# A second PSUM bank for row work in two layers, and a last group with tiles of its own

## The chip, the cores and the metric

The kernel runs on one core of one Trainium2 chip. The metric is the device time of one execution in microseconds. Its engines are TensorE (PE: matmuls, and PEld its weight loads), VectorE (DVE), ScalarE (ACT), GpSimd (POOL) and SyncE (SP, which issues the loads). PSUM is the memory that matmuls write[...].

## The reference, cut to what matters

Four graph layers work on the same 4096 nodes with 64 features and the same dense 4096 x 4096 matrix of zeros and ones. Each layer is added to its input and layer-normed.

```python
# layer 0: mean of neighbours, linear map, relu, normalize
z = concat([x, (adj @ x + x) / (rowsum(adj) + 1)]) @ W + b
x = layernorm(x + normalize(relu(z)))
# layers 1 and 3: attention between all pairs in hyperbolic space
att = sigmoid(left[:, None] + right[None, :] + b) * adj
x = layernorm(x + proj(expmap(x, einsum('ij,ijd->id', att, logmap(x_i, x_j)))))
# layer 2: each row's last neighbours with weights halving from the right
rank = cumsum(adj, axis=1); deg = rank[:, -1:]; k = minimum(deg, 100)
pos = rank - (deg - k)
w = adj * where(pos > 0, 0.5 ** (k - pos), 0)
x = layernorm(x + w @ (x @ weight) + bias)
```

A layer needs all rows of the one before it, since every row sums over all columns.

## The kernel before, in words

**Tiling.** The function `stream` works on groups `s` of 1024 rows (WW), from the last (3) to the first (0): GROUPS. Against each group it streams the matrix in 16 loads of 1 MB (`load`, L685; six buffers, issued by SP), each with two blocks of 128 columns, also from the last to the first. So each layer has 64 loads and reads the matrix once. In layer 2 the first pass (`wide_pass`) takes groups 3 and 2 together, and two `narrow_pass` take 1 and 0.

**Pair work and row work.** Pair work is what is done for every block against a group. In layer 0: matmuls into four `acc` banks (L1354), and on VectorE the test that the matrix holds only zeros and ones, one for every second load (`check`, L824), which also holds the load's buffer. In layers 1 and 3 (`attend`): three matmuls for each z half (L1045, L1048, L1051), a Sigmoid and a Square on ScalarE (L1060, L1063), two products on VectorE (L1066, L1068), and sums on PE (L1023). In layer 2: counts on PE (L1502), an Exp on ScalarE (L1509), sums on PE (L1514).

Row work is what happens to a group once its sums are there: turning them to rows, norms, the next layer's operands. It is written as generators: `end_0` and `end_2` end layers 0 and 2 (with `norm_rows` and `prepare` behind them), `move` ends layers 1 and 3, `linear` makes x @ W for layers 0 and 2 (L1207 turns x, ScalarE copies it, L1218 multiplies, then VectorE or ScalarE takes the result), `spread_left` lays out the left logits.

**Order of issue.** Generators wait in two queues. `tick(n)` is called after every step of pair work and lets each queue issue its next step; a step yields the number of ticks until the next. `need(tag)` ticks without pair work until something is done; layer 2 calls it before each quarter of the columns, since `supports` of that quarter (halves, L1228 and L1229) come from `linear(2, s)`. In layers 0 and 2 (`manual_schedule(engines=FIXED)`) PE and ScalarE keep the order in which the program issues; VectorE, POOL and SP there, and all engines in layers 1 and 3, are ordered by a planner that simulates with its own costs and takes the first instruction that is ready, the earlier issued one if there are several. In layers 1 and 3 `mark` (L597) keeps row work behind the pair work issued before it, from the second group on, until the last group's pairs are issued.

**The bank of row work.** Every matmul of row work writes a tile of the pool `aux`, which has one bank: `take` (L665) gets it and notes it in `held`; a step that has read it pops `held`; `free` (L670) makes other generators wait in the order of issue until nobody holds it. Even so the next writer waits on the chip for the last reader. In layer 0 six more banks are in use. Later the pool `ps` has three z tiles of two banks and one `acc` bank; in layer 2's wide pass two z tiles hold counts, and both halves of the third (`both`, L1445) the sums, while the `acc` bank is idle.

**The move.** `move` (L1084) is a chain of some 100 small instructions on 128 x 8 numbers with a few on 128 x 512. `Small` (L714) puts the small ones on POOL for all groups but the last, and on VectorE for the last. The products w = x * u (L1109) and x * p (L1193) are on POOL for every group. All groups share the row tiles: numbers such as `k`, `d`, `uu`, the big ones `w_att`, `sq` and `u_1`, one buffer each. In layer 3 `store` (L1533), a DMA issued on ScalarE, follows each group; the store of group 1 is issued in the same tick as the first step of group 0's move. After the last store nothing is left but a check of the input's form, which is done earlier.

Of the kernel before, what the change touches and what calls it, by code (L numbers as in the profile page):

```python
# [10 lines left out]
F32 = mybir.dt.float32  # L11
F16 = mybir.dt.float16
# [5 lines left out]
PSUM = bass.MemoryType.PSUM  # L18

P = 128  # L20
N = 4096
D = 64
NB = N // P
W = 512
# [7 lines left out]
WB = WW // P  # L32
# [26 lines left out]
def gnn_stack_kernel(  # L59
# [15 lines left out]
    nc = tc.nc  # L75
    V = nc.vector
# [11 lines left out]
    for src, at in ((b0, 0), (b2, D), (b_att1, 2 * D), (b_att3, 2 * D + 1), (r1, 2 * D + 2)):  # L88
        n = src.shape[0]
# [479 lines left out]
    def stream(fits):  # L569

        with ExitStack() as st:
# [7 lines left out]
            row = pool("f_row")  # L579
# [34 lines left out]
            def tick(n):  # L614
                for _ in range(n):
                    place[1] += 1
                    mark(False)
                    for queue in queues:
                        while queue and queue[0][1] <= place[1]:
                            wait = next(queue[0][0], None)  # L620
                            if wait is None:
                                queue.pop(0)
                                continue
                            queue[0][1] = place[1] + wait
                            if wait:
                                break
                    mark(True)

            def later(steps, second=False, wait=0):
                queues[second].append([steps, place[1] + wait])  # L630
# [30 lines left out]
            def pool_done(small, large=0):  # L661

                return 2 + int(small * 0.33 + large)

            def take(dtype, *shape):  # L665

                held.append(1)
                return aux.tile(list(shape), dtype, name="aux")

            def free():  # L670
                while held:
# [4 lines left out]
            def x_of(layer):  # L676

                if layer not in layers_x:
                    layers_x[layer] = xs.tile([P, NB, D], F32, name="x")
                return layers_x[layer]  # L680
# [10 lines left out]
            def grp(name, bufs=None):  # L691
                kw = {"bufs": bufs} if bufs else {}
                return row.tile([P, WB, D], F32, name=name, **kw)

            def nums(name, n=WB):
                return row.tile([P, n], F32, name=name)

            def over(v):
                return v[:, :, None].to_broadcast([P, v.shape[1], D])
# [14 lines left out]
            class Small:  # L714


                def __init__(self, on_pool):
                    self.on_pool = on_pool
                    eng = nc.gpsimd if on_pool else V
                    self.ts, self.mul = eng.tensor_scalar, eng.tensor_mul  # L720
                    self.add, self.sub = eng.tensor_add, eng.tensor_sub

                def stt(self, out, in0, scalar, in1, op0, op1):
                    if not self.on_pool:
                        V.scalar_tensor_tensor(out, in0, scalar, in1, op0, op1)
                        return
                    t = nums("pool_t")
                    nc.gpsimd.tensor_scalar(t, in0, scalar, None, op0)
                    nc.gpsimd.tensor_tensor(out, t, in1, op1)

# [3 lines left out]

                def rsqrt(self, a, name, small):

                    r, t = nums(name), nums("rs_t")
                    if self.on_pool:
                        yield self.wait(small)
                    V.tensor_scalar(  # L740
                        r.bitcast(I32), a.bitcast(I32), -0.5, float(0x5F3759DF),
                        ALU.mult, ALU.add,
                    )
                    for _ in range(3):
                        self.mul(t, r, r)
                        if self.on_pool:
                            self.mul(t, t, a)
                            self.ts(t, t, -0.5, 1.5, ALU.mult, ALU.add)
                            self.mul(r, t, r)
                        else:  # L750
                            self.stt(t, t, -0.5, a, ALU.mult, ALU.mult)
                            self.stt(r, t, 1.5, r, ALU.add, ALU.mult)
                    return r
# [330 lines left out]
            def move(layer, s, sums, curve):  # L1084
# [4 lines left out]
                least = 1e-15 if layer == 1 else 1e-30  # L1089
                at = blocks(s)  # L1090
                xg, x2g = x_of(layer)[:, at, :], x2[:, at]
                k, d, uu = nums("k"), nums("d"), nums("uu")
                w, sq = grp("w_att"), grp("sq")

                all_u = row.tile([P, WB, D + 1], F32, name="u_1")
                u, sum_1 = all_u[:, :, :D], all_u[:, :, D]
                for part in range(2):
                    yield from free()
# [7 lines left out]
                    )  # L1106
                    held.pop()
                    yield near()
                nc.gpsimd.tensor_mul(w, xg, u)  # L1109
                nc.scalar.activation(sq, u, AF.Square)  # L1110

                G = Small(s != GROUPS[-1])
                yield G.wait(0, 1) if G.on_pool else near()
                V.tensor_reduce(uu, sq, AX.X, ALU.add)
                yield soon()
# [73 lines left out]
                G.stt(p, p, 1.0, r, ALU.add, ALU.mult)  # L1189
                G.mul(q, q, r)  # L1190
                yield soon()
                E = nc.gpsimd if G.on_pool else V
                nc.gpsimd.tensor_mul(w, xg, over(p))  # L1193
                E.tensor_mul(u, u, over(q))
                yield soon()
                yield soon()
# [56 lines left out]
            with ExitStack() as lp:  # L1253
                own = lp.enter_context(tc.tile_pool(name="m0_own", bufs=1))
                sb = lp.enter_context(tc.tile_pool(name="m0_sb", bufs=2))
                ps = lp.enter_context(tc.tile_pool(name="m0_ps", bufs=6, space=PSUM))

                first = own.tile([P, NB, 2 * D], BF16, name="first")
                third = own.tile([P, NB, D + 1], BF16, name="third")
# [78 lines left out]
                with tc.manual_schedule(engines=FIXED):  # L1338
                    for s in GROUPS:
# [42 lines left out]
                        if s > 0:  # L1382
                            own_of = linear(0, s - 1, w0_sb[:D, :], own_part)
                            later(in_turn((0, s - 1), own_of))


            place[0] = 1
            sb = pool("p_sb", 2)
# [2 lines left out]
            def z_tile():  # L1391
                return ps.tile([P, WW], F32, name="z", bufs=3)
# [27 lines left out]
            def end_2(s, sums):  # L1420
                z = grp("z0")
                yield 1
                yield from free()
                t = to_rows_of(sums)
                yield 1
                V.scalar_tensor_tensor(
                    z.rearrange("p (h k) f -> p h k f", h=2)[:, 0], t[:, 0], 2.0**CUT / SUP,
                    b2_sb[:, None, :].to_broadcast([P, SB, D]), ALU.mult, ALU.add,
                )
                V.scalar_tensor_tensor(  # L1430
                    z.rearrange("p (h k) f -> p h k f", h=2)[:, 1], t[:, 1], 2.0**CUT / SUP,
                    b2_sb[:, None, :].to_broadcast([P, SB, D]), ALU.mult, ALU.add,
                )
                held.pop()
                yield 1
                V.tensor_add(z, z, x_of(2)[:, blocks(s), :])
                yield 1
                yield from norm_rows(3, s, z, x2[:, blocks(s)])
                yield from prepare(3, s, att3, batt3_sb, curve3, 1e-30, good[:, 1], 40)

            def wide_pass(two):

                zs = [z_tile() for _ in two]

                both = z_tile()  # L1445
                accs = [both[:, :W], both[:, W:]]
                behind, lag = [None, None], []
                for g in reversed(range(NB // 2)):
                    edges = [load_2(s, g) for s in two]
                    need((2, 2 * g // WB))  # L1450
                    for k in (1, 0):
                        j = 2 * g + k
                        w = sb.tile([P, 2, WW], F32, name="sq").bitcast(BF16)[:, :, :WW]
                        for i, edge in enumerate(edges):
                            here = edge[:, k * WW : (k + 1) * WW]
                            count(zs[i], behind[i], here, j, WW)
                            behind[i] = here
                            weights_of(zs[i], WW, w[:, i])
                            if i == 1:
                                for of, acc in enumerate(accs if lag else ()):  # L1460
                                    add_up(acc, *lag[of])
                                lag = [(j, w[:, n, :W], w[:, n, W:]) for n in range(2)]
                            if two[0] != GROUPS[0] or j < BLOCKS[4]:
                                tick(1)
                for of, acc in enumerate(accs):
                    add_up(acc, *lag[of])
                return accs
# [43 lines left out]
            def add_up(acc, j, *ws):  # L1511
                for part in range(2):
                    for h, w in enumerate(ws):
# [4 lines left out]
                            stop=j == BLOCKS[-1] and part == 1,  # L1518
                        )

            with tc.manual_schedule(engines=FIXED):

                for some in (GROUPS[:2], GROUPS[2:3], GROUPS[3:]):
                    accs = wide_pass(some) if len(some) == 2 else narrow_pass(some[0])
                    for s, acc in zip(some, accs):
                        sums = row.tile([P, W], F32, name="sums", bufs=2)
                        nc.scalar.copy(sums, acc)
                        later(end_2(s, sums))


            place[0] = 3
# [91 lines left out]
```

## Time and profile before

| | us |
|---|---|
| median of three runs | 1134.94 |
| lowest, highest | 1126.09, 1137.0 |
| the profiled execution | 1138.77 |
| its span | 1137.0 |
| PE, VectorE, ScalarE, POOL busy in it | 1027.5, 909.9, 802.1, 277.8 |

PE is busy for 90% of the span, VectorE for 80%, ScalarE for 71% and POOL for 24%. A line of a timeline has the start and the duration in us, the engine, the source line, the operation, what it writes and reads, and in brackets the engine's idle time before it and what ended it. ACTq stands for an instruction that ScalarE only issues, such as a DMA. Busy time of PE is modelled, and its matmuls overlap.

### The profile page before, as it was taken

What the parts mean: (1) busy time and instruction counts of PE and PEld (TensorE: products, weight loads), DVE (VectorE), ACT (ScalarE), POOL (GpSimd) and SP (SyncE); (2) the same over time, 40 slices, a digit from 0 to 9 for tenths busy, and PEclk for the clock granted to TensorE, in tenths of its full rate; (3) what the DMA queues carried; (4) which work ended last, traced back from release to release, by engine and by line L of the source; (5) the groups of instructions that cost most, each with busy time, mean ns of one, the idle gap of its engine ahead of it and who ended that gap; (6) DMA issues with size and microseconds to landing.
All of it is one profiled execution on the core that took longest, in us unless ns stands there. A gap on an engine that the chain in (4) does not pass through costs nothing.

```text
span 1137.0 us, 13841 instructions
## 1 busy us (share of the span) xinstructions
PE 1027.5 (90%) x4949; PEld 406.2 (36%) x4949; DVE 909.9 (80%) x1450; ACT 802.1 (71%) x896; POOL 277.8 (24%) x649
## 2 busy tenths in 40 slices
PE   5998989789999999998989998789899999999960
PEld 2554555233333333332334323223233333333320
DVE  6577976999999999989354494544999999999964
ACT  0003122989989889986755778889899999998940
POOL 0011101010145244315400020000101444345282
PEclk9989998899999999999988999799999999999985
DMA  9999999546666566553967987478546766766300
GB/s 345 395 372 385 358 416 358 184 148 223 208 236 222 185 223 221 190 210 125 367 222 262 361 274 274 145 272 286 195 158 218 253 222 199 253 219 215 133 1 22
DMA packets 38421, 271.60 MB, mean 239 GB/s; under 512 B 4550, under 2 KB 4550, under 8 KB 5574
## 3 DMA queue, kind: packets, MB, share of 16 engines
q1 hardware_dynamic: 37440, 269.50, 65.6%
q10 hardware_dynamic: 902, 1.12, 0.3%
q8 instruction: 41, 0.67, 0.2%
q14 instruction: 38, 0.31, 0.1%
HBM read 269.55 MB, written 1.05 MB: 238 GB/s over the span
## 4 chain that ended last, share of the span: by engine, by line
PE 59%; DVE 23%; ACT 8%; POOL 4%; DMA 3%; issue 2%; ACTq 0%; SPq 0%; POOLq 0%; DVEq 0%
PE acc L1023 14%; PE z L1502 9%; DVE t L1068 7%; PE z L1045 7%; DVE t L1066 6%; PE z L1051 6%; PE z L1048 6%; PE acc L1354 6%; PE z L1514 3%; DMA edges<-in_adj_dram 3%; ACT sq L1063 3%; PE acc L1514 2%; ACT sq L1509 2%; DVE junk L824 2%; ACT sig L1060 1%
## 5 line engine op out<-in xcount | busy, mean ns | idle before, releaser
L1066 DVE SCALAR_TENSOR_TENSOR t<-z,sig 128x1024 f32<-128x1024 f32 x256 | 309.6, 1219 | 16.8 <-ACT sq L1063 10.2
L1063 ACT ACTIVATE sq<-z,turn 128x1024 f32<-128x1024 f32 x256 | 278.0, 1112 | 43.8 <-PE z L1051 18.3
L1068 DVE SCALAR_TENSOR_TENSOR t<-sq,t 128x2048 f32<-128x2048 f32 x128 | 296.5, 2316 | 0.4
L1060 ACT ACTIVATE sig<-left_b,right 128x1024 f32<-128x1024 f32 x256 | 286.0, 1147 | 3.1 <-DVE t L1066 2.7
L1023 PE MATMUL acc<-t,xe 128*64 128x512 f32 x1024 | 258.6, 612 | 16.1 <-DVE t L1068 15.9
L1045 PE MATMUL z<-edges,two_i 128*128 128x512 bf16 x512 | 201.2, 393 | 6.6 <-DVE t L1066 6.6
L1051 PE MATMUL z<-dst,src 74*128 74x512 f16 x512 | 195.4, 382 | 0.0
L1048 PE MATMUL z<-lo_hi,hi_lo 128*128 128x512 f16 x512 | 194.4, 380 | 0.0
L1509 ACT ACTIVATE sq<-z,at_edge 128x512 bf16<-128x512 f32 (+1 forms) x192 | 149.9, 829 | 49.2 <-PE z L1502 46.6
L824 DVE SCALAR_TENSOR_TENSOR t<-edges 128x2048 bf16<-128x2048 f32 x32 | 73.1, 2289 | 59.2 <-DMA edges<-in_adj_dram 59.0
L1023 PEld LDWEIGHTS acc<-t,xe 128*64 128x64 f32 x1024 | 64.2, 137 | 146.7 <-issue 86.9
L1502 PE MATMUL z<-edges,pass_by 128*128 128x512 bf16 x248 | 91.5, 409 | 19.3 <-ACT sq L1509 19.3
L1354 PE MATMUL acc<-edges,first 128*128 128x512 bf16 x256 | 84.0, 411 | 13.2 <-DMA edges<-in_adj_dram 13.1
L1045 PEld LDWEIGHTS <-two_i 128*128 128x128 bf16 x512 | 50.4, 98 | 125.8 <-issue 81.2
L1502 PE MATMUL z<-edges,enter 128*128 128x512 bf16 x256 | 92.6, 404 | 0.0
L1354 PE MATMUL acc<-edges,third 128*65 128x512 bf16 x256 | 83.0, 407 | 0.0
L824 DVE SCALAR_TENSOR_TENSOR junk<-edges 128x2048 bf16<-128x2048 f32 x32 | 73.1, 2286 | 5.3 <-DMA edges<-in_adj_dram 5.1
L1051 PEld LDWEIGHTS <-src 74*128 74x128 f16 x512 | 49.2, 96 | 70.0 <-issue 8.0
L1048 PEld LDWEIGHTS <-hi_lo 128*128 128x128 f16 x512 | 50.4, 98 | 57.5 <-issue 12.1
L1109 POOL TENSOR_TENSOR w_att<-x,u 128x512 f32<-128x512 f32 x8 | 14.4, 1798 | 183.1 <-ACT u L1104 183.1
L855 POOL TENSOR_TENSOR sq<-z 128x512 f32<-128x512 f32 x8 | 14.1, 1757 | 180.3 <-DVE z L854 159.7
L1212 ACT COPY x_t<-aux 64x512 f32<-64x512 f32 x16 | 9.2, 576 | 59.2 <-PE aux L1207 59.2
(333 smaller groups left out, 1017.5 us busy)
## 6 DMA issues: line engine op xcount, KB each, us to landing
edges<-in_adj_dram SPq DMA_DIRECT2D x256, 1024.0 KB, 5.0
x<-in_x_dram SPq DMA_DIRECT2D x4, 256.0 KB
out_dram<-x ACTq DMA_DIRECT2D x4, 256.0 KB
w_sb<-in_L_gnn_W_dram ACTq DMA_DIRECT2D x1, 32.0 KB, 4.7
given<-in_L_gnn_b_dram ACTq DMA_DIRECT2D x1, 0.2 KB
given<-in_L_gnn_bias_dram ACTq DMA_DIRECT2D x1, 0.2 KB
given<-in_L_gnn_b_att_dram ACTq DMA_DIRECT2D x1, 0.0 KB
given<-in_L_gnn_att_b_dram ACTq DMA_DIRECT2D x1, 0.0 KB
```

The costliest lines, as they stand in the source:

```text
L824: V.scalar_tensor_tensor(junk, a, 0.0, a, ALU.not_equal, ALU.not_equal, accum_out=odd[:, n : n + 1])
L1023: it = nc.tensor.matmul(acc[h * D : (h + 1) * D, :], xe[:, j, :], t[:, k, h * W : (h + 1) * W], start=j == BLOCKS[0], stop=j == BLOCKS[-1],)
L1045: nc.tensor.matmul(half, two_i, edge[:, at : at + W], start=True, stop=False)
L1048: nc.tensor.matmul(half, hi_lo[:, of], lo_hi[:, to], start=False, stop=False)
L1051: last = nc.tensor.matmul(half, src[:, of], dst[:, to], start=False, stop=True)
L1060: nc.scalar.activation(sig, left_b, AF.Sigmoid, bias=right[:, j : j + 1])
L1063: nc.scalar.activation(sq[:, k], zp, AF.Square, bias=turn, scale=-1.0 / UNIT)
L1066: V.scalar_tensor_tensor(t[:, k], zp, 0.0, sig, ALU.max, ALU.mult)
L1068: V.scalar_tensor_tensor(t, sq, HIGH**2, t, ALU.add, ALU.mult)
L1354: nc.tensor.matmul(accs[h][:m], lhs[:, j, :], edge[:, at : at + W], start=j == BLOCKS[0], stop=j == BLOCKS[-1],)
L1502: nc.tensor.matmul(z[:, h : h + W], lhs, rhs[:, h : h + W], start=j == BLOCKS[0], stop=True, skip_group_check=True,)
L1509: nc.scalar.activation(w, z[:, :n], AF.Exp, bias=at_edge, scale=-LN2)
```

## The change

Three things are changed.

1. `take` alternates between `aux` and a second bank, where the list `spare` holds one. In layer 0 that is a new pool `m0_aux` of one bank. In layer 2 it is the second half of a z tile, `third_z`, that is kept through the layer; its first half takes the sums of the second group of the wide pass, and those of the first go to the `acc` bank. `spare_ends` ticks until nothing is held and goes back to one bank; it stands at the end of layers 0 and 2. `free` and `held` stay as they were.
2. The small numbers of a move go through `G.nums`, which gives the last group a set of its own (suffix `_1`). Its big tiles are `y` and `xw` in place of `w_att` and `sq`, and in layer 3 the storage of `ys` in place of `u_1` (all three are used in `prepare`, which is over by then).
3. In the last group's move the two products that stood on POOL are on VectorE.

```diff
+            spare, turn_of = [], [0]
             def take(dtype, *shape):
                 held.append(1)
-                return aux.tile(list(shape), dtype, name="aux")
+                turn_of[0] += 1
+                if not spare or turn_of[0] % 2:
+                    return aux.tile(list(shape), dtype, name="aux")
+                return spare[0](dtype, shape)
+
+            def spare_ends():
+                while held:
+                    tick(1)
+                spare.clear()
...
+                last = s == GROUPS[-1]
+                G = Small(not last, "_1" if last else "")
+                E = V if last else nc.gpsimd
+                nums = G.nums
                 k, d, uu = nums("k"), nums("d"), nums("uu")
-                w, sq = grp("w_att"), grp("sq")
-                all_u = row.tile([P, WB, D + 1], F32, name="u_1")
+                w, sq = (grp("y"), grp("xw")) if last else (grp("w_att"), grp("sq"))
+                if last and layer == 3:
+                    all_u = ys.rearrange("p k f -> p (k f)").bitcast(F32)[:, : WB * (D + 1)]
+                    all_u = all_u.rearrange("p (k f) -> p k f", f=D + 1)
+                else:
+                    all_u = row.tile([P, WB, D + 1], F32, name="u_1")
...
-                nc.gpsimd.tensor_mul(w, xg, u)
+                E.tensor_mul(w, xg, u)
                 nc.scalar.activation(sq, u, AF.Square)
...
-                E = nc.gpsimd if G.on_pool else V
-                nc.gpsimd.tensor_mul(w, xg, over(p))
+                E.tensor_mul(w, xg, over(p))
                 E.tensor_mul(u, u, over(q))
...
+                rest_ps = lp.enter_context(tc.tile_pool(name="m0_aux", bufs=1, space=PSUM))
+                spare.append(
+                    lambda dtype, shape: rest_ps.tile(list(shape), dtype, name="aux_2")
+                )
...
-                both = z_tile()
-                accs = [both[:, :W], both[:, W:]]
+                accs = [ps.tile([P, W], F32, name="acc"), third_z[:, :W]]
...
+            third_z = z_tile()
+
+            def of_third(dtype, shape):
+                t = third_z[:, W:]
...
             with tc.manual_schedule(engines=FIXED):
+                spare.append(of_third)
                 for some in (GROUPS[:2], GROUPS[2:3], GROUPS[3:]):
...
+                spare_ends()
```

`of_third` returns that half in the shape and type asked for. Layer 0's loop ends with `spare_ends()` too.

More of the change, by code (lines that the diff above doesn't have):

```diff
@@ L714, in stream, with __init__ @@
             class Small:
-                def __init__(self, on_pool):
-                    self.on_pool = on_pool
+                def __init__(self, on_pool, suffix):
+                    self.on_pool, self.suffix = on_pool, suffix
                     eng = nc.gpsimd if on_pool else V
@@ L721, in __init__, with nums @@
                     self.add, self.sub = eng.tensor_add, eng.tensor_sub
+                def nums(self, name):
+                    return nums(name + self.suffix)
                 def stt(self, out, in0, scalar, in1, op0, op1):
@@ L726, in stt @@
                         return
-                    t = nums("pool_t")
+                    t = self.nums("pool_t")
                     nc.gpsimd.tensor_scalar(t, in0, scalar, None, op0)
@@ L735, in rsqrt @@
                 def rsqrt(self, a, name, small):
-                    r, t = nums(name), nums("rs_t")
+                    r, t = self.nums(name), self.nums("rs_t")
                     if self.on_pool:
@@ L1108, in move @@
                     yield near()
-                nc.gpsimd.tensor_mul(w, xg, u)
+                E.tensor_mul(w, xg, u)
                 nc.scalar.activation(sq, u, AF.Square)
-                G = Small(s != GROUPS[-1])
                 yield G.wait(0, 1) if G.on_pool else near()
@@ L1519, in add_up @@
                         )
+            third_z = z_tile()
+            def of_third(dtype, shape):
+                t = third_z[:, W:]
+                if dtype == F16:
+                    return t.bitcast(F16)
+                n = int(np.prod(shape[1:]))
+                if len(shape) == 2:
+                    return t[:, :n]
+                names = "abc"[: len(shape) - 1]
+                return t[:, :n].rearrange(
+                    "p (%s) -> p %s" % (" ".join(names), " ".join(names)),
+                    **dict(zip(names, shape[1:])),
+                )
             with tc.manual_schedule(engines=FIXED):
+                spare.append(of_third)
                 for some in (GROUPS[:2], GROUPS[2:3], GROUPS[3:]):
@@ L1528, in stream @@
                         later(end_2(s, sums))
+                spare_ends()
             place[0] = 3
```

## The prediction

> **What bounds the kernel now.** I read the stage table first (columns: stretch, then busy time and instruction count of PE, weight loads, DVE, ACT, POOL; TensorE clock, DMA share, GB/s). Layer 0 runs to about 187 us, layer 2 from 525 to 783, the tail from 1102.
>
> ```profile
> 143.00:187.00 44.00, 39.03 (x240) 22.36 (x239) 37.45 (x109) 8.33 (x16) 6.68 (x9) 1.00 0.97 385
> 525.00:645.00 120.00, 110.26 (x578) 43.63 (x578) 60.66 (x126) 75.35 (x78) 20.95 (x53) 0.93 0.71 265
> 1102.00:1137.00 35.00, 2.99 (x11) 1.95 (x9) 14.13 (x83) 2.18 (x5) 10.79 (x30) 0.50 0.05 18
> ```
>
> Layer 0 is a DMA stage (share 0.97, so PE's gaps there are mostly cover), layer 2's first pass a PE stage (110 of 120 us), and the last 35 us belong to nobody: one serial chain. The timeline of the tail shows the hole in it.
>
> ```profile
> 1102.83 1.23 PE L1102 MATMUL aux<-centre,sums 128*128 128x130 f32 x4 [0.68 <-ACT sums L1074]
> ...
> 1110.66 1.18 POOL L1197 TENSOR_TENSOR x<-u,w_att 128x512 f32<-128x512 f32 x1
> 1111.87 0.34 ACTq L1534 DMA_DIRECT2D out_dram<-x  x1
> 1112.25 0.38 ACT L1104 COPY u<-aux 128x260 f32<-128x260 f32 x1 [9.47 <-POOL x L1197]
> ...
> 1114.36 0.63 ACT L1110 ACTIVATE sq<-u 128x512 f32<-128x512 f32 x1
> 1114.47 1.17 POOL L1109 TENSOR_TENSOR w_att<-x,u 128x512 f32<-128x512 f32 x1 [2.63 <-ACT u L1104]
> ...
> 1115.68 0.69 DVE L1116 TENSOR_REDUCE d<-w_att 128x8 f32<-128x512 f32 x1 [0.60 <-POOL w_att L1109]
> ```
>
> The last group's sums are turned at 1104.06, but ScalarE takes them out at 1112.25, when the group before it has ended on POOL. Two things stand there at once: `u_1` is still that group's, and that group's store (L1534) is ahead in ScalarE's queue. The other place is in layer 2, where `need` runs row work with no pair work between:
>
> ```profile
> 578.23 0.71 PE L1102 MATMUL aux<-centre,sums 128*128 128x130 f32 x4
> 579.46 0.63 PE L1207 MATMUL aux<-ident,x 128*64 128x128 f32 x4 [0.52 <-ACT u L1104]
> 580.76 0.71 PE L1102 MATMUL aux<-centre,sums 128*128 128x130 f32 x4 [0.67 <-ACT x_t L1212]
> 581.94 1.10 PE L1218 MATMUL aux<-w_sb,x_t 64*128 64x64 f32 x8 [0.47 <-ACT u L1104]
> 584.30 0.63 PE L1207 MATMUL aux<-ident,x 128*64 128x128 f32 x4 [1.26 <-DVE halves L1229]
> 585.60 1.97 PE L1218 MATMUL aux<-w_sb,x_t 64*128 64x64 f32 x8 [0.67 <-ACT x_t L1212]
> 587.50 1.04 PE L1502 MATMUL z<-edges,pass_by 128*128 128x512 bf16 x2
> ```
>
> Every step waits for the reader of the single `aux` bank. A block normally takes 2.90 us here (the exponentials start every 2.90), yet 578.30 to 592.38 passes for one block: 11.2 us lost. A second such burst (613.0 to 623.7, need of group 0) loses 10.7 − 2.9 = 7.8.
>
> [...]the copy of `u` ends at 579.41, L1207 starts at 579.46. [...]Here the same eight L1218 matmuls take 1.10 us, then 1.97 after the waits[...]. [...]POOL's L1162 took 2.19 us beside an L1068 where its like take 0.20.
>
> **The change, part by part.** The sum is made against the profiled execution (1138.77 us, span 1137.0, 1.8 around it). The median shown is 1134.94, 3.8 lower; I subtract the saving from the median.
>
> *Tail (layer 3, last group).* Own `_1` numbers, `y`, `xw` and `ys` instead of `w_att`, `sq`, `u_1` remove the wait for group 1's POOL work, if the copies also come ahead of its store. Then: first copy 1104.1 to 1104.5; L1102 again 1.24 (still one bank here) to 1105.75; copy 0.38, Square 0.63 to 1106.8; the product on DVE beside it (0.69 as L1194); two reductions 0.69 + 0.60 to 1108.1. From `k` to `q` the trace takes 1116.87 to 1129.70 = 12.83, unchanged on DVE: 1121.0. Then two products and the sum on DVE, 3 x 0.65: 1123.0, where 1132.04 stands. **Saved: 9.0.** The POOL products removed (1.17 and 1.56 us) are in it. What is late next is still this chain: group 1's POOL chain ends at 1111.85, hidden under it[...]; its third L740 on DVE (1104.60) is due before the new work arrives. Group 0's store and the 5 us behind x stay.
>
> *Burst at 578.* Same instructions with two alternating banks. L1102 to 578.95; L1207 at once to 579.6; L1102 needs the first copy (done 579.4) to 580.3; L1218 to 581.4; L1207 to 582.05; its copy 0.58; L1218 waits for that and for DVE's reading of its bank (about 583.0), 1.10 at full clock; 10.3 us of the trace's work to block end becomes 8 matmuls' 1.9 + 0.98: 587.0. Bounds: 2 (clock still halves) to 5.4 (592.4 − 587.0). I take **4.5**. DVE's `d`, which held the halves back behind POOL's product to 583.2, is ready earlier as well.
>
> *Burst at 613.* Only the wait of 0.93 for DVE's halves is a bank wait; those of L1218 for x_t are data. If PE keeps its clock, L1218 saves 0.87 and the next eight L1502 1.35: together 3.2; if not, 0.9. I take **2.0**.
>
> *Layer 0.* Bank waits of PE sum to some 8 us (L929 after L1317 four times at 0.8, L941 1.6, L1207 1.0 and others). But the last group's 16 loads arrive at 1 MB per 2.7 us from 143.27, so the last lands near 183.8, and PE's last work ends at 186.3. **0.5**, bounds −4 to 4.5. Below nothing because VectorE's order may change (see the slower rival).
>
> *Layer 2, what is added.* Its `acc` bank now takes half of the first pass, where two halves of a z tile did. The first L1514 (533.39 now) must wait for layer 1's last sums, copied at 538.02, and the L1502 of block 29 queue behind it on PE, and ACT's exponentials behind those. But the eight L1023 that the copy needs run at 536.03 only because PE's order put them late; with them ahead, both orders reach the second block's L1514 near 539.5. The third z tile is kept through layer 2: the narrow passes need two, but layer 3's first z products, now at 777 to 782, come after it is freed, up to 1.3 us. `spare_ends` issues at most a step or two. Together **1.5 lost**, bounds 0 to 8.
>
> *Layer 1's last group.* Two products of 1.2 to 1.6 us leave POOL for 0.69 on DVE around 582 and 603, beside a PE pass: nothing; if DVE were late there, 1.4 lost. No wait is added for anybody but DVE's own queue.
>
> Sum: 9.0 + 4.5 + 2.0 + 0.5 − 1.5 = **14.5**; 1134.94 − 14.5 = **1120.5**. On the profiled execution: 1124.3.
>
> **The rivals.** *The store stays ahead (28%).* In layer 3 ScalarE's order is the planner's, by its own costs. The store is traced before the copies and wins if the planner thinks POOL done first. For it: VectorE got `d` (1115.68) ahead of `uu`, against the traced order, so the planner thinks POOL's product done before ACT's Square; measured 1.17 against 0.63. It thinks POOL too fast. Against it: it put `sums` (1102.19) ahead of that same store, so in its plan the sums come before POOL's end. If the store stands before the first copy, the tail saves only the DVE products: 0.57 up to `k` and 0.36 at the end, 0.9; between the copies, 2.6. With 1.5: 1134.94 − 7 = 1128.
>
> *More than forecast (7%).* Layer 0 gives its 4.5, clock holds in both bursts (5.4 + 3.2), tail 9: 1134.94 − 21 = 1114.
>
> *It doesn't do what it says (7%).* `free()` still lets one bank be held at a time in issue order, so the bursts could hang on data and DVE, and the store holds the tail: 1133.
>
> *Slower (10%).* VectorE's order in layer 0 is the planner's too. DVE waits there for L1312 eight times, 23.4 us in all. With a free bank the plan may put those readings ahead of the 32 checks (L824) that free load slots; SP already waits for L824 27 times, 88.8 us. It decides when layer 0's DMA share falls from 0.92–0.99 below about 0.93 on average. If all 23.4 reach the DMA, 23.4 − 14.5 = 9 slower: 1144. Against it: DMA has six loads in flight to ride over 3 us.
>
> **How the numbers follow.** The forecast has 48%. The runs shown differ by 1% (1126.09 to 1137.0), which is what a measurement can tell from no change. Of the forecast's own 1112 to 1128, some three quarters lie beyond 1% faster (0.36), of the store rival a quarter (0.07), all of the larger gain (0.07): 0.50. The slower case lies beyond 1% with most of its part: 0.08. The rest, 0.42, is within 1%. The range takes the low end of the forecast (1111) and the store rival up to no gain (1135), leaving out some 2 in 10.
>
> **What would show it.** Tail: the first L1104 of the last group starts within 0.5 us of L1102's end, ahead of the store; no POOL work in it; x ends some 21 us after `sums` instead of 30. Bursts: L1207 directly behind L1102, PE clock near 1.0 between the exponentials of blocks 16 and 15. Layer 0: DMA share unchanged, first L1045 near 191. Wrong if the store is still in front, if checks of layer 0 move, or if PE stands still near 534 for layer 1's sums.

## The result and the profile after

| | before | after |
|---|---|---|
| median (us) | 1134.93 | 1120.41 |
| lowest, highest | 1125.21, 1137.88 | 1116.74, 1124.5 |
| ratio after / before, 95% interval | | 0.9884, 0.9866 to 0.9902 |
| span of the profiled execution | 1137.0 | 1121.7 |

By the ratio the change saves 13.2 us (11.1 to 15.2). The forecast was 1120.5. The number came true by luck: the largest step of the sum, the tail, gave 0.7 us where 9.0 stood, and other stages made up for it.

The stage table of the kernel after (stretch, busy time and instructions of PE, weight loads, DVE, ACT, POOL; TensorE clock as a share of full speed, DMA share, GB/s), with stretches that answer to those shown of before:

```profile
139.00:183.00 44.00, 39.53 (x229) 22.58 (x231) 36.23 (x108) 7.33 (x14) 6.65 (x9) 0.92 0.98 393
520.00:633.00 113.00, 102.29 (x568) 40.92 (x578) 62.34 (x128) 75.54 (x79) 18.53 (x52) 1.00 0.75 283
1088.00:1121.70 33.70, 2.75 (x11) 1.54 (x9) 15.29 (x85) 2.18 (x5) 7.82 (x27) 0.55 0.05 19
```

Layer 2's first pass takes 108.63 us from its first Exp to its first sums, instead of 116.53, and has the full clock throughout (1.00 for 0.93, in the stretches shown). The last stretch is hardly shorter than before and still holds 7.82 us of POOL work. The timeline of the tail shows why:

```profile
1089.11 0.71 PE L1126 MATMUL aux<-centre,sums 128*128 128x130 f32 x4 [0.68 <-ACT sums L1088]
...
1096.35 1.18 POOL L1218 TENSOR_TENSOR x<-u,w_att 128x512 f32<-128x512 f32 x1
1097.56 0.34 ACTq L1577 DMA_DIRECT2D out_dram<-x  x1
1097.94 0.38 ACT L1128 COPY ys<-aux 128x260 f32<-128x260 f32 x1 [8.89 <-POOL x L1218]
1098.37 1.24 PE L1126 MATMUL aux<-centre,sums 128*128 128x130 f32 x4 [8.55 <-ACT ys L1128]
...
1100.11 0.69 DVE L1133 TENSOR_TENSOR y<-x,ys 128x512 f32<-128x512 f32 x1 [9.69 <-ACT ys L1128]
```

The copy goes to `ys` now, a tile that no other group uses at that time, and still it waits 8.89 us for the `x` of group 1. The store of group 1 (L1577), which needs that `x`, stands in front of it on ScalarE. The rows of PE in the first burst of layer 2 (before: 578.23 to 587.50) show the other side:

```profile
573.53 0.71 PE L1126 MATMUL aux<-centre,sums 128*128 128x130 f32 x4
574.08 0.60 PE L1228 MATMUL z<-ident,x 128*64 128x128 f32 x4
574.77 0.71 PE L1126 MATMUL aux<-centre,sums 128*128 128x130 f32 x4
575.41 1.10 PE L1239 MATMUL z<-w_sb,x_t 64*128 64x64 f32 x8
576.44 0.63 PE L1228 MATMUL aux<-ident,x 128*64 128x128 f32 x4
577.74 1.10 PE L1239 MATMUL z<-w_sb,x_t 64*128 64x64 f32 x8 [0.67 <-ACT x_t L1233]
579.01 0.39 PE L1528 MATMUL z<-edges,pass_by 128*128 128x512 bf16 x1 [0.17 <-issue]
```

Row work writes `aux` and `z` in turn. The four waits for the bank are gone; the one left (0.67) is for data. The second L1239 takes 1.10 us instead of 1.97: PE's clock is 1.00 from 575 to 595 us here, and it was 0.50 from 584.84 to 591.67 before.

### The profile page after: what moved, and what is told of

The parts are those of the page before. It is cut to its first block, busy times and chain, and to the rows that moved or that the text cites. A ratio compares the mean times of both kernels' runs of the same rounds, so it can differ in the third digit from the quotient of the medians.

```text
span 1121.7 us, 13748 instructions
## 1 busy us (share of the span) xinstructions
PE 1006.6 (90%) x4861; PEld 401.8 (36%) x4949; DVE 911.3 (81%) x1454; ACT 801.8 (71%) x896; POOL 266.6 (24%) x645
## 4 chain that ended last, share of the span: by engine, by line
PE 57%; DVE 23%; ACT 9%; DMA 3%; POOL 3%; issue 3%; ACTq 0%; SPq 0%; POOLq 0%; DVEq 0%
PE acc L1037 14%; PE z L1528 9%; DVE t L1082 8%; PE z L1062 7%; DVE t L1080 6%; PE z L1059 6%; PE z L1065 6%; PE acc L1379 5%; PE acc L1540 3%; DMA edges<-in_adj_dram 3%; ACT sq L1077 3%; ACT sq L1535 2%; ACT sig L1074 2%; DVE junk L838 1%; PE z L1540 1%
## 5 line engine op out<-in xcount | busy, mean ns | idle before, releaser
L1059 PE MATMUL z<-edges,two_i 128*128 128x512 bf16 x462 | 181.6, 393 | 8.1 <-DVE t L1080 8.1
L838 DVE SCALAR_TENSOR_TENSOR t<-edges 128x2048 bf16<-128x2048 f32 x32 | 73.0, 2288 | 51.2 <-DMA edges<-in_adj_dram 51.2
L1528 PE MATMUL z<-edges,pass_by 128*128 128x512 bf16 x242 | 87.1, 397 | 20.3 <-ACT sq L1535 19.4
L1379 PE MATMUL acc<-edges,first 128*128 128x512 bf16 x241 | 78.6, 403 | 15.9 <-DMA edges<-in_adj_dram 15.4
L1528 PE MATMUL z<-edges,enter 128*128 128x512 bf16 x239 | 84.1, 393 | 0.4
L838 DVE SCALAR_TENSOR_TENSOR junk<-edges 128x2048 bf16<-128x2048 f32 x32 | 73.1, 2285 | 5.6 <-DMA edges<-in_adj_dram 5.3
L1540 PE MATMUL acc<-sq,halves 128*64 128x512 bf16 x384 | 61.6, 398 | 2.6 <-issue 1.6
L1133 POOL TENSOR_TENSOR w_att<-x,u 128x512 f32<-128x512 f32 x6 | 12.1, 2009 | 161.0 <-ACT u L1128 161.0
```

The source lines that it names most:

```text
L838: V.scalar_tensor_tensor(junk, a, 0.0, a, ALU.not_equal, ALU.not_equal, accum_out=odd[:, n : n + 1])
L1059: nc.tensor.matmul(half, two_i, edge[:, at : at + W], start=True, stop=False)
L1379: nc.tensor.matmul(accs[h][:m], lhs[:, j, :], edge[:, at : at + W], start=j == BLOCKS[0], stop=j == BLOCKS[-1],)
L1528: nc.tensor.matmul(z[:, h : h + W], lhs, rhs[:, h : h + W], start=j == BLOCKS[0], stop=True, skip_group_check=True,)
```

## The experiments

A single execution's profile is the sum of many stages, so each run below is read in pieces: the start of the last copy of `top` (end of layer 0), the first Exp to the first sums of layer 2 (its wide pass), the last sums of layer 2 to the first of layer 3, and from the sums of group 1 in layer 3 to the end of the last `x` (the tail; it is counted from group 1 rather than group 0, for a reason that E3 shows). Before: 188.37, 116.53, 91.99, 105.55 us; after: 183.90, 108.63, 92.96, 104.90 us.

### E1: the second bank in layer 0 alone

```diff
+                rest_ps = lp.enter_context(tc.tile_pool(name="m0_aux", bufs=1, space=PSUM))
+                spare.append(
+                    lambda dtype, shape: rest_ps.tile(list(shape), dtype, name="aux_2")
+                )
...
+                spare_ends()
```

> The kernel before with the second bank in layer 0 alone. Theory from the two traces (the bank waits hold PE, PE frees the load slots late, and the loads follow): the last copy of a top comes 4.5 us earlier and the time falls by 4 to 5 us. Rival, the step on record (the transfers set the end of layer 0, share 0.97): the time falls by 0.5 us. A second rival, that layer 0 gained only because the move's tiles changed the recorded order: no change.

Measured: ratio 0.9973 (0.9952 to 0.9993), 3.1 us saved (0.8 to 5.4). The last `top` copy stood at 182.62. That is more than the 0.5 of the prediction. The 4.5 that the traces of before and after differ by is not excluded, but a comparison of single traces is uncertain here by more than that, as E11 shows.

### E2: the second bank in layer 2 alone

```diff
-                both = z_tile()
-                accs = [both[:, :W], both[:, W:]]
+                accs = [ps.tile([P, W], F32, name="acc"), third_z[:, :W]]
...
+            third_z = z_tile()
...
+                spare.append(of_third)
...
+                spare_ends()
```

> The kernel before with the second bank in layer 2 alone, the acc bank and the third z tile with it. Theory from the two traces (wide pass 7.8 saved, narrow passes 2.9 saved, start of layer 3 1.7 lost): the time falls by 9 us. Rival, the steps on record (4.5 + 2.0 - 1.5): it falls by 5 us. If it falls by 12 or more, part of what the traces credit to layer 0 belongs here.

Measured: 0.9938 (0.9912 to 0.9964), 7.0 us saved (4.1 to 10.0), between both. The wide pass took 111.74 us here, not 108.63: its first burst (row work with no pair work between) is the same as in the kernel after, its second is not. PE's rows of that second burst, first in the kernel after:

```profile
605.45 1.10 PE L1239 MATMUL z<-w_sb,x_t 64*128 64x64 f32 x8 [0.68 <-ACT x_t L1233]
606.49 0.63 PE L1228 MATMUL aux<-ident,x 128*64 128x128 f32 x4
607.84 1.10 PE L1239 MATMUL z<-w_sb,x_t 64*128 64x64 f32 x8 [0.72 <-ACT x_t L1233]
609.11 0.39 PE L1528 MATMUL z<-edges,pass_by 128*128 128x512 bf16 x1 [0.17 <-issue]
```

and in E2:

```profile
604.93 1.10 PE L1231 MATMUL z<-w_sb,x_t 64*128 64x64 f32 x8 [0.68 <-ACT x_t L1225]
605.96 0.62 PE L1220 MATMUL aux<-ident,x 128*64 128x128 f32 x4
607.31 1.96 PE L1231 MATMUL z<-w_sb,x_t 64*128 64x64 f32 x8 [0.72 <-ACT x_t L1225]
609.61 0.63 PE L1514 MATMUL z<-edges,pass_by 128*128 128x512 bf16 x1 [0.34 <-issue]
```

The same instructions after the same two waits, 0.68 and 0.72 us: once the second set of eight matmuls takes 1.10 us (clock 1.00 from 605 to 612), once 1.96, close to the 1.97 of eight such matmuls before at a clock of 0.50, and the Exps lose about 3 us. E12 returns to this.

### E3: the last group's own tiles and its products on VectorE, alone

```diff
+                last = s == GROUPS[-1]
+                G = Small(not last, "_1" if last else "")
+                E = V if last else nc.gpsimd
...
+                w, sq = (grp("y"), grp("xw")) if last else (grp("w_att"), grp("sq"))
+                if last and layer == 3:
+                    all_u = ys.rearrange("p k f -> p (k f)").bitcast(F32)[:, : WB * (D + 1)]
...
-                nc.gpsimd.tensor_mul(w, xg, u)
+                E.tensor_mul(w, xg, u)
```

> The kernel before with the own tiles of the last group and its products on VectorE alone; no second bank. Theory, the store stays ahead on ScalarE: the copies of the last group still wait for the x of the group before, the chain from sums to x falls from 29.85 to about 28.5 us, and the time falls by 1.3 us. Rival, the step on record: the copies come right behind the sums, the chain is 21 us, and the time falls by 9 us.

Measured: 0.9987 (0.9968 to 1.0007), 1.5 us saved, not told apart from nothing. ScalarE's rows:

```profile
1100.89 0.58 ACT L1088 COPY sums<-acc 128x512 f32<-128x512 f32 x1 [8.80 <-PE acc L1037]
1110.67 0.34 ACTq L1554 DMA_DIRECT2D out_dram<-x  x1
1111.06 0.38 ACT L1128 COPY ys<-aux 128x260 f32<-128x260 f32 x1 [9.58 <-POOL x L1218]
```

The store is in front with no second bank in play. From group 1's sums the tail is 104.84 us; it is 105.55 before and 105.56 in E1 and E2. So parts 2 and 3 of the change together are worth 0.7 us. The chain from group 0's own sums misleads: it was 29.85 before, 28.54 after and 30.01 in a second execution of the kernel after, because the end hangs on group 1, wherever group 0's sums come. Group 1's move takes from its sums to its `x` 1097.53 − 1012.11 = 85.42 us beside pair work that needs 76, so its store comes after the sums of group 0.

### E4: the kernel after, with the store issued by SyncE

```diff
-                nc.scalar.dma_start(out[:, blocks(s), :], x_of(4)[:, blocks(s), :])
+                nc.sync.dma_start(out[:, blocks(s), :], x_of(4)[:, blocks(s), :])
```

> The kernel after with each group's store issued by SyncE instead of ScalarE. Theory, the store alone held the last group once it had its own tiles: the copy of ys starts within 0.5 us of the transposed sums, the chain from sums to x falls from 28.5 to 20 or 21 us, and the time is 8 us below the kernel after, 22 to 23 below the kernel before. Rival: the group before still runs on POOL[...], so that the last group's steps stretch, or SyncE's later loads wait behind the store: less than 4 us below the kernel after.

Measured: median 1112.36, ratio 0.9832 (0.9771 to 0.9894), 8 us below the kernel after by the medians, 6 by the two ratios (four executions only). From group 1's sums the tail is 97.92 us, 7.0 shorter than after. The timeline of all engines in it:

```profile
1081.59 0.71 PE L1126 MATMUL aux<-centre,sums 128*128 128x130 f32 x4 [0.68 <-ACT sums L1088]
...
1082.34 0.38 ACT L1128 COPY ys<-aux 128x260 f32<-128x260 f32 x1 [0.80 <-PE aux L1126]
...
1088.55 0.17 DVE L739 SCALAR_TENSOR_TENSOR r_t<-rs_t,r_t 128x8 f32<-128x8 f32 x1
1088.56 1.06 POOL L1214 TENSOR_TENSOR w_att<-x,p 128x512 f32<-128x512 f32 x1
1088.75 0.90 DVE L759 TENSOR_TENSOR rs_t<-r_t 128x8 f32<-128x8 f32 x1
1089.58 1.04 POOL L1215 TENSOR_TENSOR u<-u,q 128x512 f32<-128x512 f32 x1
1089.68 0.97 DVE L739 SCALAR_TENSOR_TENSOR rs_t<-rs_t,t 128x8 f32<-128x8 f32 x1
```

The copy starts 0.04 us after the turned sums end. What the tail gives against before is 7.6 us, and what is lost of the forecast's 9.0 is seen too: group 1's three products on POOL lie in the middle of group 0's chain, and beside each one small VectorE instruction takes longer (0.90, 0.97 and, behind the third, 1.03 us for 0.17; 2.4 us in all). The first two end at 1089.65 and 1090.65, their products at 1089.62 and 1090.62.

### E5: the kernel before, with the store issued by SyncE

The edit is E4's, on the kernel before.

> The kernel before with each group's store issued by SyncE, and nothing else: the last group still shares u_1, w_att and sq with the group before. Theory, two waits stand at the same place (the store ahead on ScalarE, and the tile u_1 that the group before reads until its last product): taking away the store leaves the other, the copies move by at most 1 us, and the time falls by 0 to 1 us. Rival, the store was the only real wait and the own tiles did nothing: the time falls by 8 us.

Measured: 0.9973 (0.9936 to 1.0011), medians 1.0 us apart; the tail is 105.64 us, unchanged. Rows of the timeline:

```profile
1106.87 1.18 POOL L1197 TENSOR_TENSOR x<-u,w_att 128x512 f32<-128x512 f32 x1
1108.08 0.34 SPq L1534 DMA_DIRECT2D out_dram<-x  x1
1108.08 0.38 ACT L1104 COPY u<-aux 128x260 f32<-128x260 f32 x1 [8.41 <-POOL x L1197]
```

The store is off ScalarE, and the copy waits all the same, now for `u_1`. Own tiles (with the products on VectorE) alone 0.7, the store alone nothing, both 7.6: two waits that end within 0.4 us of each other, of which either is enough to hold the copy.

### E6 and E11: the kernel before, with eight load slots in layer 0

```diff
+            more = []
+
             def load(s, g):
-                a = loads.tile([P, 2, WW], F32, name="edges")
+                a = (more[0] if more and g % 4 == 0 else loads).tile([P, 2, WW], F32, name="edges")
...
+                more.append(lp.enter_context(tc.tile_pool(name="m0_loads", bufs=2)))
...
+            more.clear()
```

> The kernel before with eight load slots instead of six in layer 0 (every fourth load into a pool of two that lives in layer 0 alone); no second bank. Three readings of layer 0: if the time in which the six slots come free sets it, and more slots ride over PE's stops, the last top copy moves from 188.4 to about 184 and the time falls by 3 to 5 us; if PE's own work with its bank waits sets it, the slots change it by less than 1 us; if the transfers run at their limit (share 0.97), it doesn't change either and GB/s stays at 380 to 390.

Measured: 0.9924 (0.99 to 0.9947), yet the last `top` copy at 186.35 in the profile, only 2.0 earlier. It was run again:

> The kernel before with eight load slots in layer 0 and one bank, as run before (8.6 us faster there by the medians, with its last top copy only 2.0 us earlier in the profile). If the slots did that, it comes again: 5 to 9 us faster. If the spread of single executions did most of it, the gain falls to 2 to 4 us, and the profile's own layer 0 ends anywhere from 181 to 188.

Measured: 0.9944 (0.9927 to 0.9961), 6.4 us saved (4.4 to 8.3), last `top` copy at 180.91. The slots do give some 6 us; what a single profile says of layer 0's end is uncertain by several us. Both profiles also have a shorter layer 1 (338.35 and 338.18 for 340.21 us, to the first Exp of layer 2) and first narrow pass (60.44 for 63.33). The short layer 1 does not belong to the slots: E1 and E4 have it without them (338.53, 338.26), and E10 lacks it with them (340.07). The narrow pass is a matter of TensorE's clock. Its table, before and in E6:

```profile
645.11:708.44 63.33, 57.60 (x311) 18.86 (x311) 44.12 (x141) 50.18 (x79) 8.91 (x16) 0.95 0.82 283
640.71:701.15 60.44, 54.85 (x311) 18.53 (x311) 43.85 (x141) 49.90 (x80) 8.93 (x16) 1.00 0.85 297
```

Every engine has the same instructions in the same order there. Before, the clock is 0.50 from 670.17 to 673.59 and from 694.07 to 697.48; in E6 it is 1.00 over the whole pass, and the pass is 2.9 us shorter. So a gain in the profiles' narrow pass says little of the slots themselves.

### E10: eight load slots and the second bank in layer 0

The edits of E1 and E6 together.

> The kernel before with the second bank in layer 0 and eight load slots there, nothing else. Read against the same kernel with eight slots and one bank, run beside it. Theory, either of the two reaches most of what there is: the two differ by less than 2 us, both 4 to 9 us below the kernel before. Rival, PE's bank waits hold layer 0 by themselves: this one is a further 3 us or more faster.

Measured: 0.9899 (0.9879 to 0.9919), 11.5 us saved (9.2 to 13.7), 5 us more than the slots alone (E11) run beside it; last `top` copy at 178.58. They add. The same stretch of layer 0 in the kernel before and in E10 (columns as above):

```profile
51.00:175.00 124.00, 113.24 (x641) 63.96 (x640) 97.48 (x274) 23.64 (x39) 15.94 (x21) 0.96 0.96 384
51.00:175.00 124.00, 117.57 (x685) 66.94 (x696) 106.71 (x303) 25.58 (x44) 19.99 (x27) 0.99 1.01 420
```

The kernels with one bank and six slots move 384 to 390 GB/s there (four profiles), those with the second bank 390 to 394 (six), with eight slots 402 and 415, with both 420 (two). A share of 0.96 meant that transfers were nearly always in flight, not that they could go no faster. Whether 420 is the most that they can do was not tried.

### E7: E4 with the last group's products on POOL

```diff
-                E = V if last else nc.gpsimd
+                E = nc.gpsimd
```

> The kernel after with the store on SyncE, and the three 128x512 products of the last group back on POOL (its own tiles kept). It prices that part of the change where nothing hides it. Theory: each product takes 1.1 to 1.2 us on POOL for 0.69 on VectorE, two of them with a change of engine before and after, so the chain is 1.5 to 2.5 us longer than with the products on VectorE. Rival: POOL is slower but beside VectorE's reductions, and the difference is below 0.7 us. If POOL is still in the group before when the first product is due, the chain is 4 us or more longer.

Measured: median 1122.85, ratio 0.9872 (0.9843 to 0.9901), 10.5 us above E4 by the medians, 4.5 by the ratios; the tail is 104.34 us, 6.4 longer than in E4. The timeline:

```profile
1097.82 1.18 POOL L1218 TENSOR_TENSOR x<-u,w_att 128x512 f32<-128x512 f32 x1
1098.95 1.18 POOL L1133 TENSOR_TENSOR y<-x,ys 128x512 f32<-128x512 f32 x1
```

The first product, ready at 1092.8, queues behind group 1's last. It was the third case of the expectation: there is a third tie to group 1, POOL's queue. So part 3 of the change, which with part 2 is worth 0.7 us in the kernel after, is worth 6.4 us once the store is out of the way.

### E8 and E9: E4 with layer 3's first Sigmoids held back, then eight slots too

In the kernel after, ScalarE's rows in the last narrow pass of layer 2:

```profile
701.48 1.27 ACT L1535 ACTIVATE sq<-z,at_edge 128x512 bf16<-128x512 f32 x2
702.76 1.28 ACT L1074 ACT_TABLE_LOAD   x1
704.06 1.15 ACT L1074 ACTIVATE sig<-left_b,right 128x1024 f32<-128x1024 f32 x1
705.22 1.28 ACT L1535 ACT_TABLE_LOAD   x1
706.52 1.27 ACT L1535 ACTIVATE sq<-z,at_edge 128x512 bf16<-128x512 f32 x2
```

The planner has put a Sigmoid of layer 3 there (three in all), and each costs two table loads.

```diff
-                        nc.scalar.copy(sums, acc)
+                        last_of_2[0] = nc.scalar.copy(sums, acc)
...
+                        with ExitStack() as hold:
+                            if layer == 3 and s == GROUPS[0] and j >= BLOCKS[3]:
+                                hold.enter_context(tc.issue_after(last_of_2[0].ins))
+                            nc.scalar.activation(
+                                sig, left_b, AF.Sigmoid, bias=right[:, j : j + 1]
+                            )
```

> The kernel after with the store on SyncE, and the first Sigmoids of layer 3 held behind the last sums copy of layer 2. In the kernel after three of them stand between the Exps of the last narrow pass, at 695 to 711, each with two table loads of 1.28 us; PE waits 2 to 3 us for each. Theory: without them the narrow pass ends 5 to 7 us earlier, the Sigmoids cost 3.4 us at layer 3's start where half of it is beside other work, and the time falls by a further 3 to 6 us, to about 1107. Rival: the work that they did ahead comes back whole at the start of layer 3, and PE or the row work sets the end of the narrow pass anyway: within 1 us of the kernel with the store on SyncE.

Measured: 1107.75, ratio 0.9746 (0.9726 to 0.9766), 4.6 us below E4 by the medians, 9.8 by the ratios. The last narrow pass falls from 73.71 to 62.79 us. Layer 3's first group takes 93.09, about as in the first profile of the kernel after (92.96), but 2.4 more than in E4 (90.68); E12 shows that one program can take either. With the edit of E6 on top:

> The kernel after with the store on SyncE, the first Sigmoids of layer 3 held behind layer 2, and eight load slots in layer 0. Theory, slots and second bank both only keep the loads running, so that either reaches most of what there is: within 2 us of the kernel with six slots (1107.75). Rival, they add: 4 us or more below it.

Measured: 1102.83, ratio 0.9708 (0.9658 to 0.9758), last `top` copy at 178.19: 32 us below the kernel before and 17 or 18 below the kernel after, by the medians.

### E12: the kernel after, again

No edit.

> The kernel after, unchanged, a second time and on another chip. It asks what belongs to the program and what to one execution. If the clock after a short wait of TensorE is a matter of the execution, its pieces take other values from the two seen so far (first pass of layer 2: 108.6 or 111.7 us; first group of layer 3: 90.7 or 93.0; layer 1: 338.3 or 340.1), and its layer 0 ends anywhere from 181 to 185. If they belong to the order of instructions, all pieces repeat to 0.1 us: 108.63, 92.96, 340.05, and layer 0 at 183.9.

Measured: 0.9853 (0.9832 to 0.9875), median 1119.61. The pieces do change, at the same order of instructions in these layers: wide pass 111.79 (108.63 in the first profile), first group of layer 3 90.68 (92.96), layer 0's end 182.80 (183.90). PE's rows in layer 3 after the same wait of VectorE, first execution:

```profile
805.94 0.59 PE L1059 MATMUL z<-edges,two_i 128*128 128x512 bf16 x1 [2.35 <-DVE t L1080]
806.32 0.63 PE L1062 MATMUL z<-lo_hi,hi_lo 128*128 128x512 f16 x1
```

and second:

```profile
809.62 0.39 PE L1059 MATMUL z<-edges,two_i 128*128 128x512 bf16 x1 [2.36 <-DVE t L1080]
809.85 0.38 PE L1062 MATMUL z<-lo_hi,hi_lo 128*128 128x512 f16 x1
```

Here it is the first execution that has the longer matmuls; in the second burst of layer 2 it had the shorter ones. The granted clock goes with them: from 800 to 825 us it is 0.86 in the first and 1.00 in the second, from 605 to 612 us 1.00 and 0.67. The waits of that burst are 0.69 and 0.72 us in E12, and the L1239 behind them takes 1.78 us for 1.10. In the profiles of before and after, every stretch at half clock but the last lasts 3.41 us or two or three times that (14 and 10 stretches). What decides whether a wait is followed by one was not shown.

## Why the prediction was right in its sum and wrong in its steps

| step | forecast | measured |
|---|---|---|
| tail | 9.0 | 0.7 (three profiles with own tiles, three with shared) |
| burst at 578 | 4.5 (2 to 5.4) | 3.6 |
| burst at 613 | 2.0 (0.9 to 3.2) | 1.1 or 4.2, by the clock |
| layer 0 | 0.5 (−4 to 4.5) | 3.1 (0.8 to 5.4) |
| layer 2's additions | −1.5 | 0 at its start; layer 3's first group −1.0 (first profile) or +1.3 (E12), by the clock |
| first narrow pass | not in the sum | 2.7 (first profile, clock 1.00 for 0.95) or 1.3 (E12) |
| layer 1's last group | 0 | 0 (layer 1 340.21 us before, 340.05 after) |

**Tail: wrong.** The step said "if the copies also come ahead of its store", and they did not. The rival "the store stays ahead" had the mechanism, the place and nearly the price (0.9; 0.7 measured). The argument for it, that a planner which put `d` ahead of `uu` thinks POOL too fast and the store ready early, fits what came; the planner's own costs were not looked at. The argument against it, that `sums` came ahead of the store, said nothing on the copies behind `sums`. (In that rival's sum the "1.5" must be 5.5, what the other steps give; its 7 is then right.) Even with the store gone the 9.0 would have been 7.6 (E4). The sum had group 1's POOL chain "hidden under it"; beside it, group 0's VectorE instructions took 2.4 us longer (E4).

**Bursts: right in kind, mis-sized.** The waits went where the prediction saw them, and PE's clock rose from 0.83 to 1.00 (575 to 595 us). From the Exp of the last block ahead of the first burst to that of the last block ahead of the second, the gain is 34.36 − 30.73 = 3.6. That is under the 4.5, and a new wait is seen there: the Tanh of the row work (L1164, at 583.64) waits 2.65 us for VectorE in front of the next Exp. From there to the first sums the gain is 34.25 − 30.04 = 4.2 in the kernel after, and in E2, where the second L1231 takes 1.96 us, 34.25 − 33.14 = 1.1; the prediction's bounds had 3.2 and 0.9 for just these two cases, so the first was 1.0 too small.

**Layer 0: mis-sized.** The step argued from a DMA share of 0.97 that the loads set the end. E10 refutes it: from 51 to 175 us it moves 420 GB/s at a share of 1.01, 9% more than the 384 that the kernel before moves at 0.96. Both the slots and PE's bank waits held the loads back, and taking away either helped. Ends of layer 0 over all profiles, averaged: one bank and six slots 185.6 (188.37, 183.04, 187.40, 183.54), second bank 182.8 (six profiles), eight slots 183.6 (two), both 178.4 (two). The 188.37 of the profile before was the latest of four, so comparing two profiles gave 4.5 where the layer gained about 3. By these ends alone the slots would not be told apart from the spread; their case rests on the rates and on the times of E11 and E10. The slower rival, VectorE's order at the tests that free the slots (L838), did not come: the share stayed at 0.96 to 0.99.

**Layer 2's additions: overestimated.** The wait for the `acc` bank exists (0.77 us before an L1540 at 531.99), but the Exps fall into step 10.2 us after the first one in both kernels: the step's argument that both orders reach the second block together was enough, and nothing had to be taken off for it. A loss of 1.0 in layer 3 came in the first profile (92.96 for 91.99) and is the clock's: the same program takes 90.68 in E12, at a clock of 1.00 throughout for 0.96.

**The sum.** E1, E2 and E3 give 3.1 + 7.0 + 1.5 = 11.6, and their intervals leave room for the 13.2 of the whole change. The forecast of 14.5 was met because the tail's missing 8.3 stood against layer 0 (+2.6), layer 2's wide pass (4.8 to 7.9 for 6.5), the 1.5 not lost, and the two narrow passes, of which the forecast had nothing. These are 1.6 to 2.8 us shorter together, nearly all of it in the first: 63.33 us at a clock of 0.95 before, 60.66 at 1.00 in the first profile of the kernel after, and 62.00 in E12. The change is not needed for it, as E6 shows. Nothing in the prediction called for these sums to cancel: that they did is luck.

## What to carry to other kernels

Where an instruction waits for something that ends at the same time as two or three other things it could be waiting for, list them all: the tile's last reader, what stands ahead in its own queue, the queue of the engine that comes next. Expect nothing until the last of them is gone. A DMA issued from a compute engine's queue is one of them: here moving it was worth nothing while the tiles were shared, and 7.0 us once they were not. A high DMA share is no proof of a limit (here 384 GB/s at 0.96, where 420 was reached): compare GB/s with the best that any run reaches in the same stretch. And take a stage's gain from several executions, or from pieces that repeat, before explaining it.

## What the runs showed of the hardware that was not expected

- TensorE's clock after short waits was not settled by the instructions alone. After waits of 0.68 or 0.69 and 0.72 us, with 1.7 us of work between, eight matmuls took 1.96 us in E2 and 1.78 in E12 (clock 0.67 from 605 to 612 us), and 1.10 in the first profile of the kernel after (1.00). After 2.35 us the next matmuls took 0.59 and 0.63 us in that profile (0.86 from 800 to 825 us) and 0.39 and 0.38 in E12 (1.00). The stretches around them differ by 2.3 us (92.96 and 90.68) and 3.1 us (33.14 and 30.04). What sets the moment at which the clock changes was not shown.
- From 51 to 175 us of layer 0 the loads reached 420 GB/s at a DMA share of 1.01 (E10), and 384 at 0.96 (before).
- In E4 128x8 instructions on VectorE, 0.17 us by themselves, took 0.90 to 1.03 us beside 128x512 products on POOL.
- Three Sigmoids between Exps cost the pass 10.9 us (73.71 to 62.79): 3 x (1.15 + 2 x 1.28) = 11.1 us of ScalarE.
